# Two rows per partition in the projections, the first keys loaded during them, and a rewritten last stage in a two-layer graph network

## The chip, the cores and the metric

The kernel runs on one core of a Trainium2 chip. The time is device microseconds of one execution; lower is better. A core has TensorE (PE, matrix products), VectorE (DVE), ScalarE (ACT), GpSimd (POOL), and 16 DMA engines that serve queues. SyncE (SP) only issues transfers here; ACT and POOL issue some as well. Each of these queues issues its work in order.

## The reference

`x` has 3327 rows (nodes) of 128 features, `adj` is a sparse 3327 x 3327 matrix of weights with a full diagonal.

```python
# layer 0
X_in  = (A / rowsum(A)) @ X @ W_in
X_out = (A.T / rowsum(A.T)) @ X @ W_out
x = layernorm(x + X_in + X_out)
# layer 1
q = (x @ Wq.T).reshape(d, n, h)      # d = 128 "heads", n = 3327, h = 8 components
k = (x @ Wk.T).reshape(d, n, h)
v = (x @ Wv.T).reshape(d, n, h)
a = einsum('dnh,dmh->dnm', q, k) * d**-0.5 + adj + adj
out = einsum('dnm,dmh->dnh', softmax(a, axis=2), v).reshape(n, h * d)
x = layernorm(x + out @ Wo.T)
```

The reshape is a plain reinterpretation of memory: the projection of a node gives 128 positions of 8 components each, and head `d` owns the 3327 positions from `d * 3327` on. A head's keys therefore come from some 26 neighbouring nodes, and a head's first position lies anywhere inside a node's row.

## The kernel before

**First stage (L137 to L177).** The rows of `adj` and then of its transpose are loaded in 26 tiles of 128 x 3327 numbers, into six buffers `a_t`, issued in turn by SP and ACT. For each tile PE adds `x0.T @ a_t` to seven PSUM banks `acc` (L153), ACT sums the rows (L151, degrees), and in the first pass counts the entries (L157) while DVE finds the 16 largest entries of each row and their places (L160 to L167). In the second pass ACT also sums the negative entries (L155, `below`), which serves a check that the matrix has the expected form. ACT copies `acc` to `yt_out` and `yt_in` (L171). Then DVE turns places into node numbers (L193 to L200), PE multiplies `yt` with `W_in` and `W_out` (`mix`, L207), DVE adds both, scaled, to `x0` (L208), and a layer norm follows (L108 to L115): statistics of all 26 tiles, one square root and reciprocal, then 26 normalising instructions. PE transposes the result to `x1t`.

**Projections (L241 to L314).** For each of 26 tiles of 128 nodes, PE computes q, k and v (L289, 128 x 1024 each). For q and k, ACT copies the product to `full` (L297), POOL rearranges it to `flat` (L299), which SP stores in `qf_d` or `kf_d` (L300), and ACT and DVE split it into three bf16 parts (`sb`, L305 to L308), which SP stores in `q_d` or `k_d` (L309): 24 rows (3 parts x 8 components) of all 425984 positions. One such store has 128 partitions x 24 rows x 128 positions. `q_d` has `G + N` columns and `k_d` has `G` (`G` is 425984, `N` 3327). For k, `mixed_keys` (L260) forms half sums and half differences of neighbouring positions on POOL, splits them too, and stores those of the first 1024 paired columns of heads 0 and 2 of each group of four in `kk_d` (L278). `paired_from` gives the column at which a head's pairs begin, so that it falls on a node. v goes to `v_d` by a POOL transfer (L293). POOL also writes constants to `ones_d`, `flatmax_d`, `near_d` and `o_d` at the start of this stage (L246 to L252). Outside the main loop a scheduler sets the order of each engine's instructions.

**Main loop (L319 to L726).** Here the order is written out by hand. For 32 groups of four heads and 7 blocks of up to 512 queries, a stream of maxima (PE products L502, ACT L512, DVE L516 and L522) runs ahead of the stream of exponentials (PE L700, ACT L710) and of the sums of shares times values (PE L668). Keys and values of a group are loaded by SP (L397; 27 or so transfers, `load_group`) into one of two buffers `k_st`; queries (12 transfers) into one of five. Before the loop proper, 2 x 38 items of maxima are computed alone. Beside all that, POOL treats the 16 neighbours of each node separately, gathered by indirect transfers, because only they have an adjacency weight; their sums go to `near_d`, those of all pairs to `o_d`, both with their own maxima.

**Last stage (L729 to L791).** For each of 26 tiles of 128 x 128 positions SP loads `o_t` (L742), `c_t` (L768) and `n_t` (L770), three buffers each; the last tile has 127 partitions. `joined` computes the gap of both maxima (L773, L774), the two factors `up` and `down` (DVE L776, L778, then ACT L779, L780), `more = n_t * down` on POOL (L782), `o_t * up + more` on DVE (L787, L788), and `divide` takes the reciprocal of the summed ninth row and scales the other eight (L762, L763). Eight PE transposes (L746), an ACT copy (L748) and 16 PE product rows (L751) give the output, which DVE adds to `x1` (L752). After all tiles the second layer norm follows, and two stores.

The lines of the code named here are these:

## Time and profile before

| | us |
|---|---|
| median of 3 runs | 13656.64 (13655.4 to 13656.82) |
| profiled execution | 13661.98 |
| its span, first to last instruction | 13660.3 |
| first stage, until the first projection | 425.7 |
| projections, until the last key store has landed | 450.3 |
| first keys and queries loaded | 41.5 |
| maxima alone | 92.5 |
| main loop | 12345.5 |
| last stage | 304.8 |

Over the span PE is busy 95%, DVE 92%, ACT 93%, POOL 39%; the mean granted TensorE clock is 0.973 of full speed. Stage borders are read from the timeline. A row of a group gives line, engine, operation, output and inputs with shapes, count, then busy time and mean time of one, then the idle time just before these instructions and what ended it. A row of a stretch of time gives the busy time of each engine with the number of instructions, the granted clock, the busy share of the 16 DMA engines (over 1 where packets overlap) and what they moved. A row of the timeline gives start, duration, engine and instruction, and in brackets the idle time before it. A row of the chain of waits gives start, duration and what was waited for.

### The profile page before, as it was taken

How to read it: one execution, taken by the hardware profiler on the slowest of the kernel's cores; microseconds unless marked ns; L12 is line 12 of the kernel's file. 1: busy time of each engine (PE TensorE's matmuls, PEld its weight loads, DVE VectorE, ACT ScalarE, POOL GpSimd, SP SyncE). 2: the span in 40 equal slices, each digit the busy share in tenths (PEclk: the TensorE clock that was granted, in tenths of full speed). 3: DMA queues.
4: the chain of work that ended last, by engine and by line, in shares of the span. 5: the costliest groups of instructions: out<-in, count | busy, mean ns of one | idle time of the engine just before them, and what ended most of it. 6: DMA issues, size and time to landing. Idle time of an engine off the chain costs nothing.

```text
span 13660.3 us, 323883 instructions
## 1 busy us (share of the span) xinstructions
PE 12915.5 (95%) x131844; PEld 3257.4 (24%) x131844; DVE 12550.7 (92%) x15861; ACT 12758.0 (93%) x24146; POOL 5383.7 (39%) x4580
## 2 busy tenths in 40 slices
PE   8649999999999999999999999999999999999994
PEld 3212222222222222222222222222222222222223
DVE  7559999999999999999999999999999999999986
ACT  7529999999999999999999999999999999999992
POOL 0420000003555555555555555555555555555002
PEclk9759999999999999999999999999999999999996
DMA  6873333333344443343334343344443443333203
GB/s 250 166 122 29 32 32 31 31 32 50 67 72 70 72 67 67 66 68 65 62 66 68 65 69 64 67 70 67 71 68 64 68 68 68 67 63 62 24 7 107
DMA packets 2714611, 929.92 MB, mean 68 GB/s; under 512 B 2437473, under 2 KB 2565600, under 8 KB 2706449
## 3 DMA queue, kind: packets, MB, share of 16 engines
q1 hardware_dynamic: 2584913, 410.90, 26.2%
q0 software_dynamic: 124176, 453.33, 12.0%
q10 hardware_dynamic: 4016, 44.88, 0.9%
q8 instruction: 1034, 16.94, 0.6%
q14 instruction: 472, 3.87, 0.1%
HBM read 786.20 MB, written 151.52 MB: 69 GB/s over the span
## 4 chain that ended last, share of the span: by engine, by line
PE 79%; DVE 9%; ACT 6%; issue 4%; DMA 1%; POOL 1%; SPq 0%; another core or an unknown queue 0%; DVEq 0%; ACTq 0%; POOLq 0%
PE o L668 39%; PE m L502 35%; PE e_ps L700 5%; DVE mx L522 5%; ACT es L710 4%; DVE larger L516 1%; DVE top_at L161 1%; DVE top_w L160 1%; POOL more L782 1%; ACT size L512 0%; ACT unread L151 0%; PE pr L289 0%; ACT o_sb L677 0%; POOL both L264 0%; DMA kk_d<-both_sb 0%
## 5 line engine op out<-in xcount | busy, mean ns | idle before, releaser
L710 ACT ACTIVATE es<-e_ps 128x512 f32<-128x512 f32 x21632 | 11445.2, 612 | 174.9 <-PE e_ps L700 123.3
L522 DVE TENSOR_REDUCE mx<-m 128x1 f32<-128x1024 f32 (+2 forms) x10816 | 10649.5, 1050 | 110.9 <-PE m L502 45.3
L700 PE MATMUL e_ps<-q_st,k_st 50*128 50x512 bf16 (+1 forms) x23296 | 6817.5, 366 | 109.3 <-ACT es L710 101.2
L502 PE MATMUL m<-k_st,q_st 48*128 48x512 bf16 (+1 forms) x23296 | 6518.0, 367 | 208.4 <-DMA q_st<-q_d 117.7
L668 PE MATMUL o<-es,v 128*9 128x256 f32 (+1 forms) x83456 | 6626.1, 389 | 5.3 <-ACT o_sb L677 5.3
L502 PEld LDWEIGHTS <-q_st 48*128 48x128 bf16 x23296 | 1423.0, 94 | 5077.6 <-issue 4940.7
L471 POOL CAST two<-nm 128x16 bf16<-128x16 f32 (+1 forms) x224 | 43.7, 195 | 5788.5 <-DVE nm L465 5788.5
L668 PEld LDWEIGHTS o<-es,v 128*9 128x9 f32 x83456 | 1243.1, 88 | 4354.7 <-issue 4333.1
L516 DVE CUSTOM_DVE_ANT_0 larger<-size,m 128x512 f32<-128x512 f32 x1664 | 1144.6, 688 | 514.9 <-PE e_ps L700 454.2
L700 PEld LDWEIGHTS <-k_st 50*128 50x128 bf16 (+1 forms) x23296 | 1402.2, 95 | 217.6 <-issue 187.7
L512 ACT ACTIVATE size<-m 128x512 f32<-128x512 f32 x1664 | 987.4, 593 | 144.5 <-PE m L502 77.5
L588 POOL TENSOR_TENSOR prod<-qn,near_rows 128x1024 f32<-128x1024 f32 x416 | 986.5, 2371 | 29.7 <-DMA qn<-qf_d 12.1
L634 POOL TENSOR_TENSOR acc<-acc,prod 128x1024 f32<-128x1024 f32 x390 | 885.6, 2271 | 30.6
L633 POOL TENSOR_TENSOR prod<-near_rows,s 128x1024 f32<-128x1024 f32 x390 | 771.7, 1979 | 7.2
L590 POOL TENSOR_TENSOR half<-prod 128x512 f32<-128x512 f32 x416 | 530.1, 1274 | 32.6
L548 POOL DMA_INDIRECT near_rows<-kn_d,near x416 | 417.4, 1003 | 110.7 <-issue 57.4
L548 POOL DMA_INDIRECT near_rows<-vn_d,near x416 | 411.9, 990 | 63.4 <-issue 22.4
L153 PE MATMUL acc<-a_t,x 128*128 128x512 f32 (+1 forms) x728 | 305.0, 580 | 66.0 <-DMA a_t<-in_adj_dram 43.8
L617 POOL TENSOR_TENSOR s<-s,gain 128x2048 f32<-128x2048 f32 x26 | 93.8, 3609 | 693.8 <-ACT s L616 693.8
L592 POOL TENSOR_TENSOR quarter<-half 128x256 f32<-128x256 f32 x416 | 254.5, 612 | 32.6
L153 PEld LDWEIGHTS acc<-a_t,x 128*128 128x128 f32 x728 | 140.8, 195 | 229.8 <-issue 181.8
L611 POOL COPY acc<-top 128x128 f32<-128x128 f32 x26 | 10.7, 413 | 467.8 <-DVE top L609 467.8
(155 smaller groups left out, 3535.3 us busy)
## 6 DMA issues: line engine op xcount, KB each, us to landing
q_st<-q_d SPq DMA_DIRECT2D x2304, 32.0 KB
a_t<-in_adj_dram ACTq DMA_DIRECT2D x13, 1663.5 KB
a_t<-in_adj_dram SPq DMA_DIRECT2D x13, 1663.5 KB
a_t<-in_adjt_dram SPq DMA_DIRECT2D x13, 1663.5 KB
a_t<-in_adjt_dram ACTq DMA_DIRECT2D x13, 1663.5 KB
q_d<-wq_sb SPq DMA_DIRECT2D x26, 768.0 KB
k_d<-wk_sb SPq DMA_DIRECT2D x26, 768.0 KB
k_st<-k_d SPq DMA_DIRECT2D x32, 623.8 KB
```

The source lines that it names most:

```text
L502: nc.tensor.matmul(m[:, at : at + width], q[64 : 64 + KR, j, i * P : (i + 1) * P], k[64 : 64 + KR, j, c0 : c0 + width], start=True, stop=True,
L512: taken = nc.scalar.activation(sizes[-1], m[:, :NB], AF.Abs)
L516: nc.vector.tensor_tensor_reduce(larger, sizes.pop(0), m[:, :NB], scale=1.0, scalar=LOWEST, op0=ALU.add, op1=ALU.max, accum_out=dst[0])
L522: reduced = nc.vector.tensor_reduce(dst[-1], src, axis=AX.X, op=ALU.max)
L548: nc.gpsimd.indirect_dma_start(rows.rearrange("p d h -> p (d h)"), None, table, bass.IndirectOffsetOnAxis(ap=near[:, t, i : i + 1], axis=0))
L588: nc.gpsimd.tensor_mul(prod, qn, kg)
L590: nc.gpsimd.tensor_add(half, prod[:, :, :4], prod[:, :, 4:])
L633: nc.gpsimd.tensor_mul(prod, vg, share)
L634: nc.gpsimd.tensor_add(acc[:, :, :H], acc[:, :, :H], prod)
L668: nc.tensor.matmul(o[32 * j : 32 * j + VW, c : c + w], v4[:pt, j, t, :], e[j][:pt, c : c + w], start=t == 0, stop=t == NT - 1,)
L700: nc.tensor.matmul(bank[:pt, j, :w], k[: KR + 2, j0 + y * per + j, t * P : t * P + pt], q[: KR + 2, j0 + y * per + j, :w], start=True, sto ...
L710: nc.scalar.activation(es[:pt, :, :w], bank[:pt, :, :w], AF.Exp, scale=2.0)
```

## The change

- First stage: `below` is the least entry of each row, found by DVE, in place of ACT's sum of negative entries. The out-going mixes, their reciprocals and updates are done tile by tile within the second pass; statistics of the first norm are taken tile by tile beside the other mixes.
- POOL's constants are written at the start of the kernel.
- Projections take 256 nodes at once: partition `p` holds nodes `2p` and `2p + 1` (`s` = 0, 1), so that a store of `q_d` or `k_d` has 128 partitions x 24 rows x 256 positions and there are 13 of each. `paired_from` gives a column at a multiple of two nodes. `kk_d` has its rows in another order. Buffers named `full`, `flat`, `left` and `parts` are shared by q and k.
- One of the key buffers and the values' buffers are allocated ahead of the projections, and the first group's loads are issued after the first 256 nodes.
- Last stage: all loads have 128 partitions. ACT makes both factors (Relu twice, one Exp for both); DVE sums the ninth row first, takes its reciprocal, multiplies both 128 x 128 factors by it, and then scales and adds the eight other rows. POOL has no part. Statistics of the second norm are taken tile by tile; the output is stored in two halves and a rest, all by SP.

The core of the diff:

```diff
 def paired_from(head):
-    return -head * N % D
+    return -head * N % (2 * D)
...
                         if name == "in":
-                            nc.scalar.activation(unread, a_t, AF.Relu, scale=-1.0, accum_out=below[:, t : t + 1])
+                            nc.vector.tensor_reduce(below[:, t : t + 1], a_t, axis=AX.X, op=ALU.min)
+                            inverse("out", slice(t, t + 1))
+                            mixed("out", t, ps_acc)
                             continue
...
                 for t in range(NT):
-                    for name in ("in", "out"):
-                        mix = ps_mix.tile([P, D], F32, name=f"mix_{name}")
-                        nc.tensor.matmul(mix, yt[name][:, t * P : (t + 1) * P], ws[f"w_{name}"], start=True, stop=True)
-                        nc.vector.scalar_tensor_tensor(
-                            x0[:, t, :], mix, recip[name][:, t : t + 1], x0[:, t, :], op0=ALU.mult, op1=ALU.add
-                        )
-                stats = big.tile([P, NT, 2], F32, name="stats")
-                layernorm(x0, stats, small, lambda t: x1[:, t, :])
+                    mixed("in", t, ps_mix)
+                    norm_stats(x0[:, t, :], stats[:, t, :], small)
+                apply_norm(x0, stats, small, lambda t: x1[:, t, :])
...
-            for t in range(NT):
-                g = slice(t * P * D, (t + 1) * P * D)
+            for t in range(NT // 2):
+                g = slice(2 * t * P * D, 2 * (t + 1) * P * D)
+                parts_of = {}
+                for name in ("wq", "wk"):
+                    parts_of[name] = stage.tile([P, PARTS, H, 2, D], BF16, name="parts", bufs=3)
+                both_sb = stage.tile([P, PARTS, 2, H, 2, D // 2], BF16, name="both_sb")
+                for s in range(2):
+                    for name in ("wq", "wk", "wv"):
+                        pr = ps_pr.tile([P, H * D], F32, name="pr")
+                        rows = x1t[:, 2 * t * P : 2 * (t + 1) * P].rearrange("d (p s) -> d s p", s=2)[:, s]
...
+                        full = stage.tile([P, H, D], F32, name="full", bufs=4)
...
+                        flat = stage.tile([P, D, H], F32, name="flat", bufs=3)
...
+                        left = stage.tile([P, H, D], F32, name="left", bufs=3)
+                        nc.scalar.copy(sb[:, 0, :, s], full)
+                        nc.vector.tensor_sub(left, full, sb[:, 0, :, s])
+                        nc.scalar.copy(sb[:, 1, :, s], left)
+                        nc.vector.tensor_sub(sb[:, 2, :, s], left, sb[:, 1, :, s])
+                        if s:
+                            nc.sync.dma_start(
+                                (q_d if name == "wq" else k_d)[:, g].rearrange("r (p c) -> p r c", p=P),
+                                sb.rearrange("p a h s c -> p (a h) (s c)"),
+                            )
+                if t == 0:
+                    group_of(0)
+                    begin_all(0)
...
-            nc.sync.dma_start(o_t[:pt], o_d[:, t * P * D : (t * P + pt) * D].rearrange("h (p c) -> p h c", c=D))
+            nc.sync.dma_start(o_t, o_d[:, t * P * D : (t + 1) * P * D].rearrange("h (p c) -> p h c", c=D))
...
-        up = small.tile([P, D], F32, name="up")
-        nc.vector.tensor_scalar_max(up[:pt], gap[:pt], 0.0)
-        down = small.tile([P, D], F32, name="down")
-        nc.vector.tensor_scalar_min(down[:pt], gap[:pt], 0.0)
-        nc.scalar.activation(up[:pt], up[:pt], AF.Exp, scale=-2.0)
-        nc.scalar.activation(down[:pt], down[:pt], AF.Exp, scale=2.0)
-        more = load.tile([P, H + 1, D], F32, name="more")
-        nc.gpsimd.tensor_mul(
+        scales = small.tile([P, 2, D], F32, name="scales")
+        nc.scalar.activation(scales[:pt, 0, :], gap[:pt], AF.Relu)
+        nc.scalar.activation(scales[:pt, 1, :], gap[:pt], AF.Relu, scale=-1.0)
+        nc.scalar.activation(scales[:pt], scales[:pt], AF.Exp, scale=-2.0)
+        sums = small.tile([P, 2, D], F32, name="sums")
+        nc.vector.tensor_mul(sums[:pt, 0, :], o_t[:pt, H, :], scales[:pt, 0, :])
+        nc.vector.tensor_mul(sums[:pt, 1, :], n_t[:pt, :, H], scales[:pt, 1, :])
+        nc.vector.tensor_add(sums[:pt, 0, :], sums[:pt, 0, :], sums[:pt, 1, :])
+        nc.vector.reciprocal(sums[:pt, 1, :], sums[:pt, 0, :])
+        nc.vector.tensor_mul(scales[:pt], scales[:pt], sums[:pt, 1:2, :].to_broadcast([pt, 2, D]))
+        nc.vector.tensor_mul(o_t[:pt, :H, :], o_t[:pt, :H, :], scales[:pt, 0:1, :].to_broadcast([pt, H, D]))
+        more = load.tile([P, H, D], F32, name="more", bufs=2)
+        nc.vector.tensor_mul(
             more[:pt],
-            n_t[:pt].rearrange("p c w -> p w c")[:, : H + 1, :],
-            down[:pt, None, :].to_broadcast([pt, H + 1, D]),
+            n_t[:pt].rearrange("p c w -> p w c")[:, :H, :],
+            scales[:pt, 1:2, :].to_broadcast([pt, H, D]),
         )
-        nc.vector.tensor_mul(o_t[:pt], o_t[:pt], up[:pt, None, :].to_broadcast([pt, H + 1, D]))
-        nc.vector.tensor_add(o_t[:pt], o_t[:pt], more[:pt])
-        divide(small, pt, o_t)
+        nc.vector.tensor_add(o_t[:pt, :H, :], o_t[:pt, :H, :], more[:pt])
...
-        nc.sync.dma_start(out[: whole * P, :].rearrange("(t p) d -> p t d", p=P), y_sb[:, :whole, :])
-        nc.scalar.dma_start(out[whole * P :, :], y_sb[: N - whole * P, whole, :])
+        for t0, t1 in ((0, NT // 2), (NT // 2, whole)):
+            nc.sync.dma_start(out[: whole * P, :].rearrange("(t p) d -> p t d", p=P)[:, t0:t1, :], y_sb[:, t0:t1, :])
+        nc.sync.dma_start(out[whole * P :, :], y_sb[: N - whole * P, whole, :])
```

## The prediction

> **What bounds the kernel now.** I read first the busy slices, then the busy time by stage, then in each short stage the wait that ends last. The profiled execution took 13661.98 us, span 13660.3; the median of the runs is 13656.64, 5.3 below. Stages, from a table of stretches (columns: window, length, then PE, weight loads, DVE, ACT, POOL busy with counts, granted PE clock, DMA share, GB/s):
>
> ```profile
> 237.50:371.00 133.50, 132.44 (x331) 62.11 (x329) 38.43 (x57) 131.77 (x87) 0.00 (x0) 1.00 0.74 268
> 371.00:393.00 22.00, 0.89 (x5) 0.87 (x5) 0.04 (x1) 21.94 (x20) 0.00 (x0) 0.60 0.01 1
> 393.00:410.00 17.00, 15.50 (x102) 14.26 (x101) 15.28 (x60) 6.39 (x5) 8.02 (x8) 0.92 0.01 2
> 410.00:425.70 15.70, 6.84 (x29) 4.52 (x29) 14.40 (x81) 4.13 (x8) 0.00 (x0) 0.67 0.00 0
> 425.70:876.00 450.30, 225.63 (x312) 74.75 (x312) 279.63 (x182) 203.75 (x208) 202.03 (x130) 0.69 1.11 193
> 876.00:917.50 41.50, 0.03 (x1) 0.06 (x2) 0.22 (x2) 0.00 (x0) 0.00 (x0) 0.50 0.70 88
> 1010.00:13355.50 12345.50, 12154.33 (x129876) 2884.30 (x129875) 11680.25 (x14621) 12170.02 (x23609) 5067.73 (x4379) 1.00 0.37 58
> 13355.50:13660.30 304.80, 130.49 (x624) 116.90 (x624) 226.10 (x313) 42.91 (x80) 101.08 (x26) 0.60 0.40 118
> ```
>
> The main loop (12345.5 us) is PE at 98%; its PE and DVE instructions stand in the same order in both kernels, so I leave it at nothing. What can change is the 1315 us around it. In the projections (425.7 to 876) no engine passes 62%, but the DMA share is over 1. Inside one 16.6 us tile:
>
> ```profile
> 594.50:596.50 2.00, 0.98 (x1) 0.50 (x2) 1.29 (x2) 1.90 (x3) 0.95 (x1) 0.50 1.04 249
> 597.00:598.50 1.50, 1.50 (x3) 0.34 (x1) 0.78 (x1) 0.69 (x1) 1.50 (x1) 0.50 1.04 346
> 601.00:604.00 3.00, 2.61 (x4) 0.52 (x2) 1.03 (x2) 0.00 (x0) 0.00 (x0) 0.50 1.42 87
> 592.60:609.20 16.60, 9.54 (x12) 3.02 (x12) 10.66 (x8) 7.80 (x8) 7.71 (x5) 0.69 1.15 201
> ```
>
> The DMA engines never rest. The first row is k_d (packets of 256 B, 249 GB/s), the second a flat table (4096 B, 346), the third q_d: also packets of 256 B, but 87 GB/s. Counted by size in the trace, 256 B packets have a median of 18 ns, 128 B 13, 4096 B 179, 4608 B 178. So one tile is: k_d 3072 x 17 ns / 16 engines = 3.3 us; two flat tables 256 x 165 / 16 = 2.6; v 128 x 178 / 16 = 1.4; kk_d 945 x 13 / 16 = 0.8; that leaves 16.6 - 8.1 = 8.5 us for q_d, 44 ns of an engine per packet. q_d's rows are (G + N) x 2 = 858622 bytes apart, no multiple of 256; k_d's 851968 is one. I take the misaligned start for the cause; the trace shows only that the two differ.
>
> In the last stage, columns of the groups being line, engine, operation, shapes and count, busy us and mean ns, idle time before; then two rows of the timeline:
>
> ```profile
> L782 POOL TENSOR_TENSOR more<-n_t,down 128x1152 f32<-128x1152 f32 (+1 forms) x26 | 101.1, 3888 | 235.5 <-ACT down L780 138.2 <-DMA o_t<-o_d 97.3
> L763 DVE TENSOR_TENSOR o_t<-o_t,rs 128x1024 f32<-128x1024 f32 (+1 forms) x26 | 50.6, 1946 | 0.0
> L751 PE MATMUL y<-wo_sb,ot 128*128 128x128 f32 (+1 forms) x416 | 87.1, 394 | 28.7 <-ACT ot L748 28.7
> ```
> ```profile
> 13596.89 0.38 DVE L773 TENSOR_TENSOR gap<-n_t,c_t 127x128 f32<-127x128 f32 x1 [10.47 <-DMA n_t<-near_d]
> 13627.77 1.36 DVE L787 TENSOR_TENSOR o_t<-o_t,up 127x1152 f32<-127x1152 f32 x1 [26.58 <-DMA o_t<-o_d]
> ```
>
> Tiles follow each other every 9.15 us, DVE and POOL slowing each other: L763 needs 1.21 us alone and 3.93 beside L782. The last tile, of 127 rows, waits 10.5 + 26.6 us for loads that the others get in 7.
>
> **First stage.** Removed: 26 ACT Relu passes (3.1 us each, 81 in all). ACT ran behind, and the copies of yt_in ended at 392.1 though PE had its sums at 371. Added on DVE: 26 least entries of 3327 columns; the row nearest is the 1024-column maximum, 1050 ns, so 3.5 us each, plus three one-column instructions (0.5 with their waits) and one update (0.26) per tile: 4.3 x 26 = 112. DVE has 36 us of gather (L193, L199, L200) and some 5 of small work there already, so it ends at 237.5 + 153 = 390, and PE, with 26 mixes (0.3 us each) more, at about 378. PE and copies hide under DVE now. Then 26 mixes with statistics interleaved, 0.6 us each (0.26 + 0.34): 406; reciprocal, normalising and transposes as before, 8.4 (before: 417.3 to 425.7): the first projection at about 415 instead of 425.7. **-10**; between -22 (DVE hides) and +5.
>
> **Projections.** Two rows per partition make q_d's and k_d's packets 512 B, half as many, and kk_d's 256 B; flat tables and v stay. For 256 rows: flats 5.3 us, v 2.9, kk_d 1.0. k_d: the last stage's 512 B packets have a median of 27 ns, so 3072 x 27 / 16 = 5.2. q_d is the disputed term. Trainium skill, "DMA: Bandwidth & Descriptors", Specifications: a transfer should be at least 512 B for line rate, and below that the engine reads, modifies and writes. By that rule q_d and k_d both go to the 346 GB/s of the large packets, 4.5 us each, and DMA needs 18.2 us per 256 rows. The rows speak against it: k_d has 249 GB/s at 256 B, so size is not what hurts q_d. If the surcharge of 27 ns (44 - 17) is for a packet's two ragged ends, q_d costs 3072 x (27 + 27) / 16 = 10.4; if it goes with the bytes, 17. The 2048 B packets of o_d, also misaligned, have 113 ns in the main loop against 93 for x0's aligned ones: a surcharge of that size, not eight times it. I take 10.4, so DMA needs 24.8 us per 256 rows (33.2 before).
>
> Compute for 256 rows: DVE 14 instructions at a pitch of 1.14 plus the measured slowing by POOL (10.66 - 8.6 per tile): 21 us. ACT 16 x 0.95 = 15. PE 24 rows at 0.5 us warm or 0.945 cold: 12 to 22.7. Following the after order of ACT and DVE through one pair with these pitches gives 18 us without slowing. So DMA stays the bound, closely; with three shared parts buffers the k half waits until the q half before it has landed, for which I add 3: **28 us**, bounds 23 (compute alone) and 34.5 (q_d by bytes, plus 3). 13 x 28 = 364, plus the fill of 18.7 there is now (450.3 - 26 x 16.6): 383 instead of 450.
>
> Moved in: the first group's keys and values, 27 loads that stand on SP directly behind the first k_d store. They wait for its landing (8 us), and all stores of the second pair, flat tables first, are queued behind them on SP; POOL's copies and ACT then wait for free flat and parts buffers. Their packets cost 13312 x 12 ns + 288 x 550 + 914 x 60 = 23 us of the 16 engines. +31, less the pair that compute runs ahead: **+30**, between +10 and +50. The stage ends at 415 + 383 + 30 = 828, instead of 876: **-38** besides the start.
>
> **Handover**, 876 to 917.5. The chain of waits:
>
> ```profile
> 867.25 8.60 DMA k_d<-wk_sb
> 878.34 7.84 DMA k_st<-k_d
> 887.35 7.46 DMA k_st<-kk_d
> 896.22 7.00 DMA k_st<-k_d
> ```
>
> Those loads are gone from here; the ones rows of k_st1 (1.2 us, half of 2.3) and the queries (909.25 to 917.44, with waits 9.3) stay. 41.5 becomes 10.5: **-31**. The 92.5 us of first maxima behind it are DVE's and unchanged. Moved off POOL, the small constants (L246 to L252) go to where POOL idles: nothing. The kk_d loads in the main loop use a three-level source; they are 24 packets, loaded a group ahead: nothing.
>
> **Last stage.** L782 leaves POOL, and all DVE instructions run at their undisturbed pitch: two gaps 0.3 + 0.2, three sums 0.2 + 0.3 + 0.2, reciprocal 0.87, scales 0.3, two products and a sum of 1024, x2 0.2, statistics 0.3. Two of the large ones take 1.13. The third reads n_t at a stride of 40 bytes: L773, which does so, takes 0.37 for 128 columns against 0.28 for L774, so +0.72, 1.9. The Trainium skill, "SBUF", says that each step to another 16-byte line costs extra, which speaks against moving this product; by a contiguous rate it would be 1.13, the sum 6.3 instead of 7.1. I keep the row. But a loop closes first: sum (1.2), transposes (1.94 cold, 1.04 warm), copy (1.0), output products (3.79 or 2.05), x2, which stands ahead of the next tile's sum on DVE: 8.35 us cold, 5.8 warm. PE had a clock of 0.60 here; at about 0.7 some 40% are warm: 0.6 x 8.35 + 0.4 x 7.1 = **7.8 us a tile**, 203 for 26. Loading 128 rows removes the 37 us of waits. Begin 10, last tile's tail 7.5, reciprocal and normalising 7.5, final store 9 (12 before; half of it starts earlier): 237 instead of 304.8: **-68**, between -90 and -45.
>
> Sum: -10 - 38 - 31 - 68 = -147; profiled 13662 - 147 = 13515, and for the median about **13510**.
>
> **The rivals.** (B) The misaligned store is cured by length: DMA falls to 18 to 20 us and compute sets 23 us a pair: 13 x 5 = 65 less, 13445. For it the 512 B rule, against it k_d's rate. (C) The surcharge goes with the bytes: 34.5 us a pair, +85, 13595. For it: 87 GB/s is a rate; against it the 2048 B packets. (D) Slower: a 512 B misaligned packet costs far more than two of 256 B. Place: q_d. The change pays until one pair takes 28 + 147 / 13 = 39.3 us, that is until q_d takes 10.4 + 11.3 = 21.7 of them, 113 ns a packet, 2.6 times now; at 130 ns, 3.3 us a pair more, 13700. Nothing in the profile shows such a step. That nothing happens would need the last stage's 37 us of load waits to stay too, which 128-row loads exclude.
>
> **How the numbers follow.** My case 0.52, B 0.27, C 0.18, D 0.02, no change 0.01. A run tells 0.2% (27 us) from no change. My own range is 13460 to 13560; with B, and C up to its middle, 13425 to 13592. Faster 0.97, same 0.01, slower 0.02.
>
> **What would show it.** Projections: a period of 28 us per pair with DMA share over 1, and q_d's stretch again near or above 87 GB/s but not at 249; at 23 us and a share below 1, B. Directly after the first pair, 25 to 35 us in which SP issues k_st loads. First PE product for the maxima about 10 us after the last k_d landing. Last stage: no POOL rows, no wait over 8 us at its end, DVE waiting on PE for x2. DVE, not ACT, last in the first stage. A changed rate in the main loop would break the prediction, and so would a second wait that the loads bring with them.

## The result, and the profile after

The kernel after takes 13541.27 us (median of 4 runs, 13536.22 to 13573.19) against 13656.51 for the kernel before beside it (4 runs, 13655.4 to 13656.82): ratio 0.9921, 95% interval 0.9903 to 0.9938. Its profiled execution took 13540.9, with a span of 13539.2, 121.1 shorter than before. The forecast was 13510; of the 147 us that it summed up, 121 came.

The stretches of the kernel after, with the same columns as those of before in the prediction (window, length, then PE, weight loads, DVE, ACT and POOL busy with counts, granted PE clock, DMA share, GB/s):

```profile
237.50:409.00 171.50, 141.29 (x382) 69.93 (x381) 144.49 (x196) 76.68 (x51) 0.00 (x0) 0.91 0.57 209
409.00:437.50 28.50, 22.09 (x84) 15.79 (x83) 23.33 (x107) 8.72 (x16) 0.74 (x1) 0.70 0.00 1
437.50:855.00 417.50, 196.89 (x312) 72.66 (x312) 306.76 (x182) 205.98 (x208) 229.64 (x132) 0.73 0.86 215
855.00:863.00 8.00, 0.08 (x1) 0.11 (x2) 0.22 (x2) 0.00 (x0) 0.00 (x0) 0.50 0.26 69
955.00:13295.30 12340.30, 12149.43 (x129878) 2882.02 (x129875) 11678.14 (x14621) 12172.25 (x23610) 5067.94 (x4379) 1.00 0.36 58
13295.30:13539.20 243.90, 135.66 (x624) 121.17 (x624) 197.22 (x365) 48.20 (x106) 0.00 (x0) 0.60 0.50 150
```

Against the rows of before, and with the first maxima product (862.92 instead of 917.47) and the last store of `o_d` as borders:

| stage | before | after | difference | predicted |
|---|---|---|---|---|
| first stage, to the first projection | 425.7 | 437.5 | +11.8 | -10 |
| projections | 450.3 | 417.5 | -32.8 | -38 |
| handover to the first maxima | 41.5 | 7.9 | -33.6 | -31 |
| maxima alone and main loop | 12438.0 | 12432.4 | -5.6 | 0 |
| last stage | 304.8 | 243.9 | -60.9 | -68 |

One stage went the other way. In the timeline of TensorE's products in the second pass of the kernel after (start, duration, instruction, idle time before it) the place is plain:

```profile
235.50 16.47 PE L190 MATMUL acc<-a_t,x 128*128 128x512 f32 x41
282.18 0.79 PE L175 MATMUL mix<-w_out,yt_out 128*128 128x128 f32 x2 [30.21 <-DVE x L176]
282.77 8.41 PE L190 MATMUL acc<-a_t,x 128*128 128x512 f32 x14
```

TensorE, which was busy for 132.4 of 133.5 us in this pass before, stops for 30.2 us in front of the second mix. Its sums are complete at 409 and no longer at 371.

TensorE's and VectorE's instructions of the main loop are the same in all kernels of this study. From the first maxima to the last store of `o_d` it took between 12426 and 12474 us in their profiles, also on other chips, where the kernel before took 13662 to 13687. So the 5.6 us can't be told from this scatter, and a total can't tell less than some 20 us apart; in what follows each experiment is read by the length of the stage that it touches. These repeat better: the first projection of seven kernels with an unchanged first stage came between 435.3 and 437.5, and the last stage of seven kernels that leave it unchanged took 238.3 to 243.9. From the first projection to the first maxima, the unchanged kernel took 425.5 here, 423.2 on the chip of the first four experiments, and 431 to 433 on the two chips of the others, so there I compare on one chip.

### The profile page after: what moved, and what is told of

Same layout as the page of the kernel before. It is cut to its first block, busy times and chain, and to the rows that moved or that the text cites. A ratio compares the mean times of both kernels' runs of the same rounds, so it can differ in the third digit from the quotient of the medians.

```text
span 13539.2 us, 323799 instructions
## 1 busy us (share of the span) xinstructions
PE 12894.4 (95%) x131844; PEld 3261.1 (24%) x131844; DVE 12646.1 (93%) x16015; ACT 12688.5 (94%) x24120; POOL 5309.1 (39%) x4554
## 4 chain that ended last, share of the span: by engine, by line
PE 80%; DVE 9%; ACT 5%; DMA 2%; issue 2%; POOL 1%; SPq 1%; DVEq 0%; ACTq 0%; POOLq 0%
PE o L716 38%; PE m L550 35%; PE e_ps L748 5%; DVE mx L570 5%; ACT es L758 4%; DVE larger L564 1%; PE acc L190 1%; DMA q_d<-parts 1%; DVE top_at L200 1%; PE y L800 1%; DVE top_w L199 1%; ACT size L560 0%; SPq L340 0%; DMA kf_d<-flat 0%; POOL prod L636 0%
## 5 line engine op out<-in xcount | busy, mean ns | idle before, releaser
L636 POOL TENSOR_TENSOR prod<-qn,near_rows 128x1024 f32<-128x1024 f32 x416 | 986.6, 2372 | 28.4 <-DMA qn<-qf_d 13.0
L682 POOL TENSOR_TENSOR acc<-acc,prod 128x1024 f32<-128x1024 f32 x390 | 885.7, 2271 | 30.6
L188 ACT ACTIVATE unread<-a_t 128x3327 bf16<-128x3327 f32 x52 | 155.0, 2980 | 103.0 <-PE acc L190 38.3
```

The lines of the kernel that those rows point to most:

```text
L636: nc.gpsimd.tensor_mul(prod, qn, kg)
L682: nc.gpsimd.tensor_add(acc[:, :, :H], acc[:, :, :H], prod)
```

## The experiments

**1. Is it the start of a packet that makes `q_d` slow?** In the kernel after, and then in the kernel before, `q_d` gets two more columns, so that its rows start on multiples of 512 bytes:

```diff
-    q_d = dram.tile([PARTS * H, G + N], BF16, name="q_d")
+    q_d = dram.tile([PARTS * H, G + NP], BF16, name="q_d")
```

> The kernel after, with q_d two columns wider (G + NP instead of G + N), so that its rows lie 858624 bytes apart, 1677 x 512, and every packet of a q_d store starts on a multiple of 512 bytes. Theory 'misaligned start': the 3072 q_d packets of a pair fall from about 54 ns to the 27 of k_d, q_d's transfer from 10.4 to about 5.2 us a pair, DMA needs some 20 us a pair and the computing engines set the period at 23 to 24 us instead of 27.6: projections shorter by 40 to 55 us, total about 13495. Rival 'something other than alignment makes q_d slow' (its place in the queue, its size): the period stays within 0.5 us of 27.6 and the total within 10 us of the kernel after, 13541. Rival 'compute already sets 27.6': packets get shorter, the DMA share falls, the period stays.

> The kernel before with the same two columns added to q_d and nothing else. Theory 'misaligned start': q_d takes 3.3 us of a tile's 16.6 instead of 8.5, DMA needs 11.4, and the period falls to between 11.4 and 13.5 us (compute with its queues may close first): projections 80 to 130 us shorter, total 13530 to 13575, so that this edit alone is worth more than the longer packets were. Rival 'not alignment': period 16.6, total within 10 us of 13657.

The first: 13519.66 us (4 runs; kernel before on this chip 13662.24; ratio 0.989, 0.9874 to 0.9907). The second: 13642.01, ratio 0.9982 (0.9968 to 0.9995). The rows of the steady part of the projections, first before and before with wider `q_d`, then after and after with wider `q_d`:

```profile
500.00:860.00 360.00, 179.29 (x224) 57.27 (x223) 228.26 (x151) 167.97 (x172) 161.04 (x104) 0.66 1.15 196
```
```profile
500.00:860.00 360.00, 183.59 (x224) 58.79 (x224) 232.09 (x154) 169.09 (x174) 164.57 (x104) 0.65 0.67 202
```
```profile
526.70:830.00 303.30, 151.09 (x224) 53.91 (x224) 251.37 (x146) 166.13 (x168) 193.31 (x105) 0.75 0.92 238
```
```profile
522.30:810.00 287.70, 145.63 (x224) 53.29 (x224) 248.05 (x146) 165.78 (x167) 189.31 (x105) 0.78 0.81 251
```

The packets do get shorter. Counted by size in the traces, the 256 B packets of before fall from a mean of 31.8 ns to 15.6, the 512 B packets of after from 36.9 to 28.8. Half of each are `q_d`'s; if `k_d`'s cost what all cost once aligned, a misaligned packet took 2 x 31.8 - 15.6 = 48 ns at 256 B and 2 x 36.9 - 28.8 = 45 ns at 512 B. These are estimates, since packets of other sizes got shorter too (those of 4096 B in before from 287 to 163 ns), but the prediction's row with 87 GB/s gives the same: 16 engines x 256 B / 87 GB/s = 47 ns. The start is the cause of the 87 GB/s, as the prediction took it.

But the time hardly follows. The DMA share of before falls from 1.15 to 0.67, and from the first projection to the first maxima it takes 470.7 us for 491.8, where I had expected to win 80 to 130 us. Where these 21 us lie is seen from ACT's last copy of k (a row of the chain of waits) and the last store of `q_d` (a row of the timeline), in before and in before with wider `q_d`:

```profile
820.60 1.02 ACT wk_full L297
859.50 0.49 SPq L309 DMA_DIRECT2D q_d<-wq_sb  x1
```
```profile
820.62 1.02 ACT wk_full L297
840.52 0.55 SPq L309 DMA_DIRECT2D q_d<-wq_sb  x1
```

The 26th copy comes 394.9 us after the first projection in before and 393.8 with the wider `q_d`, and from the fifth copy on they follow each other every 16.05 and 16.06 us. The computing engines kept one and the same pace at a share of 1.15 and at one of 0.67. Only the stores, 16.8 us apart in before (456.8 to 859.5 in 24 tiles) and 16.0 with the wider `q_d`, fell behind it, until the last one was issued 38.9 us after the last copy instead of 19.9. (For a store of `q_d` to land ACT waited 7.7 us in all.) In the kernel after, the period is 27.6 us a pair of tiles (256 nodes; 526.7 to 830.0 in 11 pairs), and 26.1 with the wider `q_d`. So the DMA engines, though full, did not set the pace of the computing engines before, nor most of the period of after. What did is in the timeline of the kernel before with wider `q_d`:

```profile
629.08 1.02 ACT L297 ACTIVATE wk_full<-pr 128x1024 f32<-128x1024 f32 x1
631.06 1.35 DVE L306 TENSOR_TENSOR wq_left<-wq_full,wq_sb 128x1024 f32<-128x1024 f32 x1 [0.63 <-ACT wq_sb L305]
632.44 1.04 ACT L307 CAST wq_sb<-wq_left 128x1024 bf16<-128x1024 f32 x1 [1.41 <-DVE wq_left L306]
633.40 1.02 ACT L297 ACTIVATE wq_full<-pr 128x1024 f32<-128x1024 f32 x1
634.47 3.78 PE L289 MATMUL pr<-wv,x1t 128*128 128x512 f32 x4 [0.53 <-ACT wq_full L297]
638.28 1.23 DVE L292 COPY v_sb<-pr 128x1024 f32<-128x1024 f32 x1 [1.99 <-PE pr L289]
639.42 1.22 DVE L268 SCALAR_TENSOR_TENSOR both_left<-both,both_sb 128x1024 f32<-128x1024 f32 x1
640.67 1.04 ACT L269 CAST both_sb<-both_left 128x1024 bf16<-128x1024 f32 x1 [5.32 <-DVE both_left L268]
645.67 1.02 ACT L297 ACTIVATE wk_full<-pr 128x1024 f32<-128x1024 f32 x1
651.05 1.98 PE L289 MATMUL pr<-wv,x1t 128*128 128x512 f32 x4 [0.89 <-ACT wq_full L297]
```

It is a ring through the engines' orders. ACT copies k out of PSUM (629.08), splits q, copies q out (633.40), and that frees the place into which PE puts v (634.47). DVE copies v (638.28) and only behind it takes the rest of the half sums (639.42), for which ACT has stood 5.3 us (640.67) ahead of the next split and the next copy of k (645.67). From copy to copy that is 16.59 us, with PE's four products at 3.78; the round that follows has them at 1.98 and takes 14.79. No engine is busy for two thirds of it. The kernel before has the same ring, with copies of k at 594.45, 611.04 and 627.64, and about every third round at 14.8 us; there the aligned store could win only the lag of the stores.

**2. Flat tables: more places, or another engine.** On the aligned kernel after, first six places for `flat` instead of three:

```diff
-                        flat = stage.tile([P, D, H], F32, name="flat", bufs=3)
+                        flat = stage.tile([P, D, H], F32, name="flat", bufs=6)
```

> The aligned kernel (q_d two columns wider) with six places for the flat tables instead of three. In the aligned kernel the chain runs over GpSimd's flat copy and the 12 to 13 us landing of a flat table, 26.1 us a pair. Theory 'places for the flat tables set the period': GpSimd no longer waits for landings, the period falls to 23.5 to 24.5 us, near VectorE's 22.5 of busy time, projections 20 to 30 us shorter than the aligned kernel's, total about 13495. Rival 'the order over four engines sets it': the period stays within 0.5 of 26.1, total within 6 us of 13520.

The waits of the copy L411 for landings fell from 38.9 us to 5.4 (50.3 us of idle time for which the trace shows no releaser stand in their place), and the period stayed, at 26.2 (523.1 to 810.9 in 11 pairs). The total was 13536.61 (kernel before there 13687.32; ratio 0.988, 0.9857 to 0.9903). From the first projection to the first maxima it took 402.6, 29 less than the unmodified stage on that chip, where the alignment alone had saved 19 on another; whether the places add to it is not settled by that.

Then ACT in place of GpSimd for these copies, in a kernel that changes three stages (its first and last stage follow below):

```diff
-                        nc.gpsimd.tensor_copy(flat, full.rearrange("p h c -> p c h"))
+                        nc.scalar.copy(flat, full.rearrange("p h c -> p c h"))
```

> Again three stages. First stage: all least entries as sums of Relu on ScalarE, as before, but the out-mixes in the pass as in the kernel after: ScalarE ends the pass at about 392 as before, VectorE is idle enough that TensorE's wait of 30 us is gone, and behind the copies only 26 mixes with their statistics (16 us) and 8.4 remain: first projection at 412 to 420; if the wait of TensorE stays over 15 us, the place for the mix is the cause and not the least entries. Projections: q_d aligned, the flat tables' copies on ScalarE (1.0 to 2.0 us each) and not on GpSimd, which leaves VectorE undisturbed by them: if GpSimd's copies and what they cost VectorE set 26.1 us a pair, it falls to 21 to 24 and the stage from 396.7 to 345 to 375; if the order over the engines sets it, it stays at 26 or grows. Last stage as in the run beside it, 211 to 217.

The total was 13524.66 (ratio 0.9882, 0.9865 to 0.9898). The period was 26.4 us (542.5 to 832.6 in 11 pairs), although VectorE had been freed, and from the first projection to the first maxima it took 401.4. Two groups of VectorE, between 500 and 780 us, of the aligned kernel and of this one (busy us, mean ns):

```profile
L371 DVE SCALAR_TENSOR_TENSOR left<-both,both_sb 128x1024 f32<-128x1024 f32 x20 | 44.2, 2209 | 0.0
```
```profile
L370 DVE SCALAR_TENSOR_TENSOR left<-both,both_sb 128x1024 f32<-128x1024 f32 x19 | 23.1, 1218 | 0.0
```

The same instruction takes 2.21 us beside GpSimd's copies and 1.22 without them; VectorE is busy 58% of the time now (161.3 of 280 us), ACT 76%. So neither VectorE's load nor the places for the flat tables sets some 26 us a pair. That leaves an order over engines like that of before; for the kernel after I have not traced that ring, and which instruction of it one should move stays open.

**3. What the early key loads are worth.** The kernel after without the four lines behind the first pair, so that the keys are loaded after the projections as before:

```diff
-                if t == 0:
-
-                    group_of(0)
-                    begin_all(0)
```

> The kernel after, with the first group's keys and values loaded behind the projections, as before, and not behind the first pair of tiles. By the prediction (loads cost 30 us where they now stand, save 31 at the handover): projections 27 to 30 us shorter, handover 41 instead of 7.9, total within 6 us of 13541. Rival 'the early loads are hidden under the fill of the projections': projections less than 10 us shorter, total 20 to 33 us longer. Rival 'they stop the queue for longer than they save': projections over 40 us shorter, total 10 us or more below 13541.

The total was 13544.81 (ratio 0.9908, 0.9891 to 0.9924). The two stretches, projections and handover:

```profile
437.30:828.00 390.70, 194.52 (x312) 71.92 (x312) 310.80 (x184) 205.08 (x208) 228.84 (x132) 0.76 0.86 224
828.00:862.00 34.00, 0.16 (x1) 0.13 (x2) 0.00 (x0) 0.00 (x0) 0.00 (x0) 0.50 0.76 83
```

The last store of `q_d` is issued 360.6 us after the first projection, and 392.5 in the kernel after: the loads cost 31.9 where they stand. From that store to the first maxima it is 63.9 and 32.9: they save 31.0. (Against the first kernel of experiment 4, on the same chip as this one, with 390.8 and 32.4, it is 30.2 and 31.5.) Both terms were foreseen at 30 and 31; together this part of the change is worth nothing. In the kernel after one sees the 39 us on SP's queue:

```profile
484.17 9.62 SPq L340 DMA_DIRECT2D k_st<-kk_d  x4
...
520.79 2.49 SPq L340 DMA_DIRECT2D v<-v_d  x2
523.39 1.96 SPq L412 DMA_DIRECT2D qf_d<-flat  x1
```

Next, the same loads two at a time behind each store of v, from the second pair on:

```diff
+                            for _ in range(2):
+                                if t and 0 in coming:
+                                    begin(0)
```

> The kernel after, with the first group's loads of keys and values not all together behind the first pair but two at a time behind each store of v from the second pair on. Loads all together held the stores of the second pair back by some 30 us (with the loads at the end the projections were 32 us shorter and the handover 33 longer). Theory 'it is the queue, not the bytes': spread, they cost 27 times 0.2 to 0.4 us, so that the projections keep 20 to 30 us of the 32 and the handover stays at about 8: total 13511 to 13521. Rival 'it is the bytes': their 23 us of DMA time comes on top, the projections stay within 10 us of 417, total 13531 or more.

The total was 13550.06 (ratio 0.9891, 0.9867 to 0.9914). From the first projection to the first maxima it took 424.7, against 431.3 and 432.6 of the two kernels on the same chip with loads at one place: 7 us, a quarter of what I hoped for. That the misaligned stores left the DMA engines little room is likely, not shown. With both edits, in the kernel that also splits the first stage (experiment 4):

> Three stages changed at once, each read by its own length. First stage: the least entries of the even tiles as sums of Relu on ScalarE as before, those of the odd tiles on VectorE; mixes in the pass as in the kernel after. If VectorE's load is what held TensorE, its wait shrinks to under 15 us, and the first projection is at 405 to 420 instead of 437; if one place for the mix alone is enough to hold it, the wait of 30 us stays and the first projection is at 430 or later. Projections: q_d aligned and the first group's loads spread; with the DMA share at 0.81 the loads' 23 us now have room: 365 to 380 from first projection to last store landed, instead of 396.7 with the alignment alone; if it is the queue that binds, 390 or more. Last stage: x2 two tiles later, 211 to 217. Total with all three good about 13541 - 25 - 40 - 22 = 13455.

The total was 13513.24 (ratio 0.9872, 0.9856 to 0.9889). The stretch took 394.3, 37.5 less than the unmodified stage on that chip, and the last three pairs, with no loads left, 24.0 us each (24.6 in the aligned kernel alone). From first projection to the last store landed it was 387, short of the 365 to 380 expected. Alignment alone had saved 19 and spreading alone 7, on other chips. On the chip of that alignment both together, in the last kernel of experiment 4, took 394.8, 28.4 less than the unmodified 423.2 there: about the sum of the two, so that they support each other is not shown.

**4. The first stage.** First the out-mixes back behind the pass, with the least entries still on VectorE:

```diff
                             nc.vector.tensor_reduce(below[:, t : t + 1], a_t, axis=AX.X, op=ALU.min)
-                            inverse("out", slice(t, t + 1))
-                            mixed("out", t, ps_acc)
                             continue
...
                 for t in range(NT):
+                    mixed("out", t, ps_mix)
                     mixed("in", t, ps_mix)
```

> The kernel after, with the inverse of the out-degrees and the 26 out-mixes taken out of the second pass over the matrix and done in the loop behind it, where they were before; the least entries stay on VectorE. Theory 'the 30 us in which TensorE waits for VectorE's update of x0 made the first stage longer': TensorE has its sums at about 371 again, the copies of yt_in end before 395, VectorE ends its least entries at about 385 and then has 26 x (0.26 + 0.26 + 0.34) = 22 us: first projection at 405 to 415 instead of 437.5, total 13541 - 22 to 32 = about 13514. Rival 'the least entries on VectorE are the cause': VectorE ends last either way, first projection at 435 or later, no gain.

The total was 13530.65 (ratio 0.9899, 0.9883 to 0.9916). The first projection is at 425.2: 12.3 sooner than in the kernel after (10 to 12 by what this stage varies), and no sooner than before (425.7). The wait for L176 is gone, another one of 8.4 us is there (rows of the matrix come late, since their buffers wait for VectorE's least entry), and the chain of waits ends with 31 us of mixes:

```profile
272.66 27.61 PE L190 MATMUL acc<-a_t,x 128*128 128x512 f32 x64 [8.37 <-DMA a_t<-in_adjt_dram]
```
```profile
380.58 3.32 ACT yt_in L208 x7
384.88 31.04 PE mix L175 x100
```
```profile
400.00:425.20 25.20, 22.53 (x79) 17.00 (x78) 20.63 (x83) 4.13 (x8) 0.72 (x1) 0.55 0.00 1
```

The copies of `yt_in` end at 383.9, 8.2 us sooner than before (392.1): with the least entries on VectorE, ACT is no longer last. The mixes take that back. Here 100 of TensorE's products need 31.0 us, and the granted clock from 400 on is 0.55; in the prediction's row of before from 393 to 410, 102 of them need 15.5 us at 0.92. The order differs too, as the statistics now stand between the mixes; what slowed them was not tested.

The mixes in the pass cost 12. In the kernel after, the second mix takes the place of the first in PSUM. VectorE's update, which empties it, stands behind the gather and behind five least entries, of which this is the last:

```profile
278.28 3.59 DVE L192 TENSOR_REDUCE below<-a_t 128x1 f32<-128x3327 f32 x1
281.80 0.33 DVE L176 SCALAR_TENSOR_TENSOR x<-mix,recip_out,x 128x128 f32<-128x128 f32 x1
```

Would more places help? Four quarters of a PSUM bank for four mixes:

```diff
-                mix = ps.tile([P, D], F32, name="mix")
+                if t % 4 == 0:
+                    mix_of[name] = ps.tile([P, 4, D], F32, name="mix")
+                mix = mix_of[name][:, t % 4, :]
```

> The kernel after, with the mixes of four tiles in turn in the four quarters of one PSUM bank (as many banks as before, four places instead of one). Theory 'one place for the mix ties TensorE to VectorE's queue': the 30 us wait of TensorE for L176's line behind the gather goes, since four mixes can be written ahead; TensorE has its sums at about 371 + 8 = 379, VectorE comes last at about 390 and the first projection at 413 to 421 instead of 437.5: total about 13541 - 20. Rival 'TensorE waits whatever the places, because 26 mixes stand in its order ahead of sums that VectorE's queue holds up for longer': a wait of 15 us or more stays and the first projection is at 428 or later.

```profile
282.18 0.79 PE L179 MATMUL mix<-w_out,yt_out 128*128 128x128 f32 x2 [30.62 <-DVE x L180]
```

Nothing was won: the wait of 30.6 us stands where it stood, for the same update, and the first projection is at 440.8 (total 13561.8; ratio 0.9911, 0.9883 to 0.9939). As VectorE's order stayed the same, and the second mix waited all the same for the first update, the four quarters were waited for as one place. What four separate places would do was not tried.

In the kernel of experiment 2 with all least entries on ACT again and the mixes in the pass, the wait is there too:

```profile
274.56 0.80 PE L175 MATMUL mix<-w_out,yt_out 128*128 128x128 f32 x2 [31.14 <-DVE x L176]
```

The gather alone is enough to hold it. And as everything behind it is late, ACT with its two passes per row becomes last, at 429, and the first projection comes at 459.3, 22 later than in the kernel after: with the mixes in the pass, the least entries on VectorE are a gain. With half of them there (the kernel that spreads the loads) the wait was 32.4 and the first projection at 453.4, against my 405 to 420.

Last, the order: the mix of tile t when row t + 8 is read, together with the aligned store, the spread loads and the later x2 of experiment 5:

```diff
+            LATE = 8
...
-                            mixed("out", t, ps_acc)
+                            if t >= LATE:
+                                mixed("out", t - LATE, ps_acc)
...
+                    if t >= NT - LATE:
+                        mixed("out", t, ps_mix)
                     mixed("in", t, ps_mix)
```

> First stage: the least entries on VectorE and the mixes in the pass, as in the kernel after, but the mix of tile t only when row t + 8 is read, and the last eight behind the pass. In TensorE's order the second mix then stands behind ten rows of the matrix and not behind four and a half, so that VectorE has the gather and the first update of x0 behind it. If the wait of 30 us came from this order (one place for the mix, and its reader behind the gather), it is under 6 us, TensorE has its sums at 380 to 386 and the first projection is at 414 to 422, instead of 437 with all mixes in the pass and 425 with all behind it; if a wait of 15 us or more stays, the first projection is at 430 or later and the order is not the cause. Projections with q_d aligned and the first group's loads spread: 390 to 398 from the first projection to the first maxima, as in the run before that had both (394). Last stage with x2 two tiles later: 214 to 218. Total 13460 to 13490, some 60 below the kernel after.

The total was 13483.18 (5 runs, 13480.39 to 13488.66; ratio 0.9866, 0.9848 to 0.9883), the shortest time of all, though the ratio can't be told from the 0.9872 of the kernel with both edits in experiment 3. Its first stage, though, missed what I expected:

```profile
272.84 19.20 PE L192 MATMUL acc<-a_t,x 128*128 128x512 f32 x42 [7.09 <-DMA a_t<-in_adjt_dram]
316.62 0.80 PE L177 MATMUL mix<-w_out,yt_out 128*128 128x128 f32 x2 [18.78 <-DVE x L178]
```

The wait became one of 7.1 for a row and one of 18.8 for an update that stood behind three of VectorE's least entries and parts of the gather (297.8 to 316.2), and the first projection is at 440.1. So it isn't the gather's place in the order alone. In all these runs with mixes between the sums, TensorE, which has no slack in this pass, stood while VectorE was behind, whatever VectorE was busy with. Of the first stages tried, that with the mixes behind the pass is the best; it was not run together with the other edits, where by the stage lengths it would take 440.1 - 425.2 = 15 us more off.

**5. The last stage.** x2 and its statistics two tiles later:

```diff
-            nc.vector.tensor_add(x2[:pt, t, :], x1[:pt, t, :], y[:pt])
-            norm_stats(x2[:, t, :], stats[:, t, :], small)
+            done.append((t, pt, y))
+            if t > 1:
+                finish(*done.pop(0))
```

> The kernel after, with x2 and its statistics of a tile done two tiles later in the last stage (three places for y in PSUM), so that VectorE does not stand and wait for TensorE before the next tile's sum. Theory of the prediction 'the loop over TensorE and back sets the period when its clock is low': the period falls from 8.08 to VectorE's own sum, about 7.1, and the last stage by 20 to 27 us, total about 13517. Rival 'VectorE's sum sets the period': it stays within 0.2 of 8.08, no change of the total beyond 5 us.

The total was 13540.47, on a chip where the kernel before took 13687.32 (ratio 0.9883, 0.986 to 0.9906); the stage itself:

```profile
13323.25:13541.80 218.55, 118.59 (x624) 105.42 (x624) 189.33 (x365) 51.09 (x106) 0.00 (x0) 0.69 0.56 167
```

218.6 instead of 239.3 to 240.5 of the three kernels with an unchanged last stage beside it (and 217.8 to 220.1 in the three other kernels with this edit), and a period of 6.95 us (`more` at 13423.56 and at 13430.52), which is VectorE's own sum (it is busy throughout); its waits for y fell from 20.7 us to 6.2. In the kernel after, two periods in the chain of waits and three groups show the loop:

```profile
13387.70 1.95 PE tr L795 x8
13389.67 1.02 ACT ot L797
13390.74 3.80 PE y L800 x16
13394.54 1.55 issue
13396.08 1.95 PE tr L795 x8
```
```profile
L837 DVE TENSOR_TENSOR more<-n_t,scales 128x1024 f32<-128x1024 f32 (+1 forms) x26 | 51.4, 1977 | 0.0
L842 DVE TENSOR_TENSOR o_t<-o_t,more 128x1024 f32<-128x1024 f32 (+1 forms) x26 | 31.7, 1218 | 0.0
L801 DVE TENSOR_TENSOR x<-x,y 128x128 f32<-128x128 f32 (+1 forms) x26 | 7.5, 287 | 20.9 <-PE y L800 20.7
```

One round is 1.95 + 1.02 + 3.80 + 1.55 and small gaps, 8.38 us, at TensorE's low clock, for which the prediction had 8.35. Last, the last tile's loads with 127 rows again:

```diff
-            nc.sync.dma_start(o_t, o_d[:, t * P * D : (t + 1) * P * D].rearrange("h (p c) -> p h c", c=D))
+            nc.sync.dma_start(o_t[:pt], o_d[:, t * P * D : (t * P + pt) * D].rearrange("h (p c) -> p h c", c=D))
```

(and `c_t` and `n_t` in the same way)

> The kernel after, with the last stage's loads of o_t, c_t and n_t cut to pt rows again, so that the last tile loads 127 rows as before; nothing else. By the prediction the waits of the last tile were the 127 rows' own price: two waits of 10 and 26 us come back at the end, the last stage is 30 to 37 us longer than the 237 to 244 of the kernel after. Rival 'they came from the transfers of that moment (the queue, GpSimd's use of memory)': the last stage stays within 8 us.

The total was 13600.96 (2 runs; ratio 0.9938, 0.9918 to 0.9958). The stage took 280.2, 36 to 42 more than with 128 rows. The two waits on VectorE, and the stretch of the first load:

```profile
13532.50 0.38 DVE L823 TENSOR_TENSOR gap<-n_t,c_t 127x128 f32<-127x128 f32 x1 [23.31 <-DMA n_t<-near_d]
13563.45 0.29 DVE L830 TENSOR_TENSOR sums<-o_t,scales 127x128 f32<-127x128 f32 x1 [17.64 <-DMA o_t<-o_d]
```
```profile
13505.00:13530.00 25.00, 5.73 (x24) 5.06 (x24) 4.12 (x11) 1.84 (x4) 0.00 (x0) 0.57 0.06 24
```

A DMA share of 0.06 is one engine of 16: the 127 packets of 5120 B follow one another, 201 ns each, for 25 us, and then the 1143 of `o_t` for 31. The Trainium skill states this in "DMA: Bandwidth & Descriptors", section "Why a DMA increments its semaphore by 16 and not by 1": the transfer is dealt to the largest number of engines up to 16 that divides the outer dimensions, and 127 partitions get one. The trace agrees.

## Why the prediction was right, and where it was not

The total lay in the range, 31 us above the forecast, with the right sign in three of the four stages that were to change. By its steps:

- **First stage, -10 (bounds -22 to +5): +11.8.** The step that failed is "PE and copies hide under DVE now": TensorE had its sums at 409 and not at 378, and the mixes behind the pass began at 412.6 and not at 390, to take the 16 us foreseen. Its durations were near (VectorE's last least entry ended at 392.4 for 390, one took 3.6 us for 3.5; without mixes in the pass VectorE ends its least entries at 367, as 237.5 + 36 + 26 x 3.6 gives). It counted 0.3 us of TensorE for each mix and no wait. It should have asked who empties the one place of `mix`, and what is queued ahead of that reader: on VectorE the gather and five least entries, hence 30.2 us of TensorE with no slack to hide them. With the mixes behind the pass the wait was gone and the first projection came 12 us sooner, but still 10 us behind the forecast of 415, after the slow mixes of experiment 4. The stage is 22 of the 26 us by which the sum of stages was too good.
- **Projections, -38: -32.8, with the mechanism half wrong.** The period of 28 us was met by 27.6, and the DMA need of 24.8 a pair by 25.2 (277.7 us of 16 engines in 11 pairs). The surcharge of a misaligned 512 B packet was 16 ns, not 27: `q_d` took 8.6 us a pair (3072 x 45 / 16), not 10.4. But "DMA stays the bound" does not hold: with 4 us a pair less for the engines the period fell by 1.4. Nor did the compute estimate of 18 to 23 us: the wider `q_d` leaves 26.1. The two errors met in a right number, which is luck. "What bounds the kernel now" erred in the same way: a share of 1.15 meant full queues, while a ring over the engines' orders set 16.05 us a tile. Of the gain, some 65 us without the key loads (450.3 to 417.5 - 31.9), most comes, it seems, from the new order and buffers of the engines' work, since the aligned kernels differ by 2 x 16.0 - 26.1 = 5.9 us a pair, 77 in 13; which of the new things brings it was not tested. The fill was larger than I took it, 417.5 - 13 x 27.6 - 31.9 = 26.8 and not 18.7.
- **Key loads, +30 and -31: +31.9 and -31.0.** As worked out, and as worthless as worked out.
- **Handover, -31: -33.6.** Right; no part was measured apart but the loads.
- **Main loop, 0:** -5.6, inside what it varies by.
- **Last stage, -68: -60.9.** Both mechanisms were shown, the loop over TensorE and the 127 rows. `more` at its stride took 1.98 us, for 1.9, against 1.22 for the contiguous sum of the same size (L842). What GpSimd's leaving the stage brought was not measured apart. The period was 8.08 (13315 to 13517 in 25 tiles) for 7.8: the clock over the stage was 0.60 and not 0.7, so that more of the tiles ran at the low one; 26 x 0.28 = 7 us, the whole miss. In the other profiles the stage is 238 to 241.
- **The rivals.** B, cured by length: fell, a misaligned packet of 512 B is slower than an aligned one, and compute does not close at 23. Nor is the 512 B rule seen here: aligned packets of 256 and of 512 B move 16.4 and 17.8 B a ns. C, by bytes: fell, the surcharge per packet shrank with length. D, a step up: fell, 45 ns is far from the 113 at which it would have decided.

## What to carry to other kernels

Before a product is put among others on a full engine, find who empties its output and what stands in that engine's queue ahead of the emptying: that backlog, not the product's own time, was its price here. A busy share of DMA over 1 says that transfers wait, not that anyone waits for them; the proof is to make them cheaper, or to follow one period round the engines' orders until it closes. A load taken off the path at one place was paid at the next, since the queue that now issues it feeds the path there.

## What the runs showed of the hardware

A store whose packets start off the boundary took 48 ns for 256 B and 45 for 512, against 15.6 and 28.8 aligned: here the start decided and the length hardly mattered. The Trainium skill, "DMA: Bandwidth & Descriptors", "How a descriptor splits into AXI transactions", says that a piece that doesn't start on a multiple of 256 bytes has its first transaction start at the boundary below. I estimate from this one transaction more, 2 for 1 and 3 for 2, and ratios of 2 and 1.5, where the runs have 3.1 and 1.6, for stores, while the page speaks of reads. And GpSimd's copies stretched a VectorE instruction on two SBUF inputs from 1.22 to 2.21 us, without that deciding the period.
